# Tap spectra of a graph-network convolution with the cosine table stationary, and its scratch stored by frequency

## The chip, the core and the metric

The kernel runs on one core of one Trainium2 chip. The metric is device time in microseconds; the time before is the median of three runs. A profile is one further look at an execution by the hardware profiler: it records every instruction on every engine and every packet of a transfer. TensorE (PE), VectorE (DVE), ScalarE (ACT), GpSimd (POOL) and SyncE (SP) run side by side, each in the order of its own queue, and sixteen DMA engines move the data. Transfers are issued from SP's and ScalarE's queues.

## The reference, cut to what matters

```python
h = relu(layernorm(x))                     # x: 128 graphs x 128 nodes x 256 channels
xc = transpose(h, (0, 2, 1))
y = relu(bn1(conv1(xc)))                   # 1x1 convolution
y = bn2(conv2(y, pad=8))                   # 17 taps along the nodes, 256 -> 256 channels
x_conv = transpose(relu(y + xc), (0, 2, 1))
# message passing, a GRU cell on [x_conv, x_nmp] and h, residual
# a second layer: five small graph convolutions over subsets of 25 nodes, residual
```

The change concerns `conv2` alone, and of it the part that depends only on the weights: the spectrum of its 17 taps.

## The kernel before

`conv2` is done by spectra. Each graph's 128 nodes are cut into two windows of 80 (64 outputs and a margin of 8 on each side), so a spectrum has `LW = 80` real numbers: cosines and sines of 40 frequencies. The kernel computes the spectra of the inputs (X), the spectra of the taps (V, 80 x 256 x 256 numbers, 21 MB, written to the DRAM scratch `vd`), multiplies them frequency by frequency, and stores the products in `yd`, which a later stage turns back.

The work has these stages, for graphs in blocks of four (`BB`):

- Heads, for the first half of the graphs (`heads`, L266): for each block a load of x (`head_load`, L184), the statistics on VectorE (`head_stats`, L193 to L198), the normalisation (`head_norm`, L204), transposes on TensorE with ScalarE's eviction (`head_turn`, L214, L215, and a store of `htd` at L216), the 1x1 convolution (`head_conv1`, L228; VectorE L231, ScalarE L232) and the spectra of the block (`head_spectra`, L243, evicted at L249 and L251). Between these steps `some_spectra` (L376) adds one group of tap spectra at a time, two or three to a block.
- Tap spectra (`weight_spectra`, L160), only beside the heads of the first half. Taps come in tiles `w2` of 1 MB (`taps_load`, L152), eight of them, each for 128 input channels and 64 output channels, 17 taps on each of four groups of 32 partitions, the other 15 rows of a group being zeros in DRAM. A group of spectra is 16 matmuls (L167): 17 rows of taps are stationary, and the 80 columns of the cosine and sine table `gt` stream; four banks are filled, one per row group. ScalarE evicts three of them (L175), VectorE the fourth (L173; in the last group of a tile ScalarE takes all four). Four groups fill a tile `sp`, which ScalarE's queue stores into `vd` (L177).
- The products (`spectral`, L287), half by half: for every two frequencies a tile v is loaded by two transfers of 512 KB (L296), GpSimd adds its two parts (L311), TensorE multiplies (L304, L314, L319), and yd is stored from ScalarE's queue (L323).
- The rest (messages, gates, second layer), which the change doesn't touch. The only lines of it used below are the large stage's L649 (gates), L914 (500-column matmuls), L767 (a small transfer of 53 or 60 rows that lays a table of degrees out anew) and the loads of yr (L471).

What sets the order around the change: in the block from L362 to L409 the program order is kept on every engine as written (`tc.manual_schedule()`), so each engine runs the lines in the order of the calls. The taps of the first three tiles are loaded from SP's queue among the first loads of x; those of the further tiles are issued from ScalarE's queue (L383), each when the spectra of an earlier tile are done, just after the store of that tile and just before the copies of the next group. The tiles `w2` have three buffers and `sp` two. PSUM has eight banks, shared by all (`bank`, L93).

The lines that a sentence can't say:

```python
 167  nc.tensor.matmul(ps[r][:, j * LW:(j + 1) * LW], w2[32 * r:32 * r + KW, 4 * t + j, :],
 168                   gt[32 * r:32 * r + KW, :], start=True, stop=True)
 296  nc.sync.dma_start(v[:, c], vd[c, :, :, 2 * p:2 * p + 4, :].rearrange("q i d o -> i q d o"))
 380  if spectra and next(spectra[0], STOP) is STOP:
 381      spectra.pop(0)
 382      if len(todo) > 2:
 383          taps.append(taps_load(wp, *todo[2], nc.scalar))
```

Of the kernel before, what the change touches and what calls it, by code (L numbers as in the profile page):

```python
# [8 lines left out]
F32 = mybir.dt.float32  # L9
# [4 lines left out]
P = 128  # L14
EPS = 1e-5
KW = 17
# [3 lines left out]
OUTW = 64  # L20
LW = 80
NP_ = LW // 2
WCH = 64
NR = 2 * LW - P
PARTS = [40, 40, 40, 8]
NN = 25
# [49 lines left out]
def gnn_kernel(ctx: ExitStack, tc: tile.TileContext, io, out0: bass.AP, out1: bass.AP):  # L76
    nc = tc.nc
    x, adjT = io["x"], io["adjT"]
    B, N, D = x.shape
    C = D // P  # L80
# [9 lines left out]
    dram = ctx.enter_context(tc.tile_pool(name="dram", bufs=1, space=bass.MemoryType.DRAM))  # L90
    psum = ctx.enter_context(tc.tile_pool(name="psum", bufs=8, space=bass.MemoryType.PSUM))

    def bank():  # L93
        return psum.tile([P, 512], F32, tag="bank", name="bank")
# [6 lines left out]
    gt = hc.tile([P, LW], F32)  # L101
# [44 lines left out]


    htd = [dram.tile([P, C, T], F32, tag=f"ht{i}", name=f"htd{i}") for i in range(NBLK)]
    vd = dram.tile([C, D // WCH, P, LW, WCH], F32, tag="vd", name="vd")
    yd = [dram.tile([HG, 2, LW, D], F32, tag=f"yd{h}", name=f"yd{h}") for h in range(NH)]  # L150

    def taps_load(pool, c, q, queue, split=1, amid=None):  # L152
        w2 = pool.tile([P, WCH // 4, P], F32, tag="w2", name="w2", bufs=3)
        for t in range(0, WCH // 4, WCH // 4 // split):
            queue.dma_start(w2[:, t:t + WCH // 4 // split], io["w2t"][:, c, q, t:t + WCH // 4 // split])
            if amid:
                amid.pop()()
        return w2

    def weight_spectra(pool, c, q, w2):  # L160

        sp = pool.tile([P, LW, WCH], F32, tag="sp", name="sp", bufs=2)
        for t in range(WCH // 16):
            ps = [bank() for _ in range(4)]
            for j in range(4):
                for r in range(4):
                    nc.tensor.matmul(ps[r][:, j * LW:(j + 1) * LW], w2[32 * r:32 * r + KW, 4 * t + j, :],  # L167
                                     gt[32 * r:32 * r + KW, :], start=True, stop=True)
            for r in range(4):
                o0 = t * 16 + 4 * r  # L170
                dst, s = sp[:, :, o0:o0 + 4], ps[r][:, :4 * LW].rearrange("p (j d) -> p d j", j=4)
                if r == 3 and t < WCH // 16 - 1:
                    nc.vector.tensor_copy(dst, s)  # L173
                else:
                    nc.scalar.copy(dst, s)  # L175
            yield
        nc.scalar.dma_start(vd[c, q], sp)  # L177


    xs, stats, hcs, h1s = {}, {}, {}, {}  # L180
# [1 line left out]
    def head_load(pool, ahead, i, queue):  # L182
        xs[i] = pool.tile([P, BB, D], F32, tag="ln", name="ln", bufs=ahead)
        queue.dma_start(xs[i], x[i * BB:(i + 1) * BB].rearrange("b n d -> n b d"))  # L184
# [102 lines left out]
    def spectral(bp, X, h, amid):  # L287

        for p0 in range(0, NP_, 4):
            amid.get(p0, lambda: None)()  # L290
            ys = bp.tile([P, 4, 2, D], F32, tag="ys", name="ys", bufs=2)
            for p in range(p0, p0 + 4):
                if p % 2 == 0:
                    v = bp.tile([P, C, D // WCH, 4, WCH], F32, tag="v", name="v", bufs=3)
                    for c in range(C):
                        nc.sync.dma_start(v[:, c], vd[c, :, :, 2 * p:2 * p + 4, :].rearrange("q i d o -> i q d o"))  # L296
                vr, vi = v[:, :, :, 2 * (p % 2), :], v[:, :, :, 2 * (p % 2) + 1, :]
                a, d = X[:, :, p, 0, :], X[:, :, p, 1, :]
                y = ys[:, p - p0]
                ps = bank()  # L300
                if p == 0:
                    for k, (u, w) in enumerate(((a, vr), (d, vi))):
                        for c in range(C):
                            nc.tensor.matmul(ps[:, k * D:(k + 1) * D], u[:, c], w[:, c], start=c == 0, stop=c == C - 1)  # L304
                    nc.scalar.copy(y.rearrange("p k o -> p (k o)"), ps)
                    continue

                s = bp.tile([P, C, P], F32, tag="s", name="s", bufs=2)
                nc.vector.scalar_tensor_tensor(s, a, -2.0, d, op0=ALU.mult, op1=ALU.subtract)  # L309
                vs = bp.tile([P, C, D // WCH, WCH], F32, tag="vs", name="vs", bufs=3)  # L310
                nc.gpsimd.tensor_tensor(vs, vr, vi, op=ALU.add)  # L311
                p1 = bank()
                for c in range(C):
                    nc.tensor.matmul(p1[:, :D], a[:, c], vs[:, c], start=c == 0, stop=c == C - 1)  # L314
                k1 = bp.tile([P, D], F32, tag="k1", name="k1", bufs=2)
                nc.scalar.copy(k1, p1[:, :D])  # L316
                for k, (u, w) in enumerate(((s, vi), (d, vr))):
                    for c in range(C):
                        nc.tensor.matmul(ps[:, k * D:(k + 1) * D], u[:, c], w[:, c], start=c == 0, stop=c == C - 1)  # L319
                nc.vector.tensor_tensor(y, ps.rearrange("p (k o) -> p k o", k=2),  # L320
                                        k1[:, None, :].to_broadcast([P, 2, D]), op=ALU.add)
            for w in range(2):
                nc.scalar.dma_start(yd[h][:, w, 2 * p0:2 * p0 + 8, :].rearrange("g d o -> g (d o)"),  # L323
                                    ys[w * HG:(w + 1) * HG].rearrange("p a k o -> p (a k o)"))
# [29 lines left out]
    with front as es:  # L354
# [7 lines left out]
        with ExitStack() as ws:  # L362

            ws.enter_context(tc.manual_schedule())

            xk = ws.enter_context(tc.tile_pool(name="xk", bufs=1, side="right"))
            wp = ws.enter_context(tc.tile_pool(name="wp", bufs=1))
            ahead = 5
            todo = [(c, q) for c in range(C) for q in range(D // WCH)]
            nc.scalar.dma_start(gt, io["gt"])  # L370
            nc.scalar.dma_start(vec, io["vec"])

            taps = [taps_load(wp, *todo[0], nc.sync, split=4, amid=[lambda: head_load(xk, ahead, 0, nc.sync)])]
            spectra = []

            def some_spectra(k=1):  # L376
                for _ in range(k):
                    if not spectra and todo:
                        spectra.append(weight_spectra(wp, *todo.pop(0), taps.pop(0)))
                    if spectra and next(spectra[0], STOP) is STOP:  # L380
                        spectra.pop(0)
                        if len(todo) > 2:
                            taps.append(taps_load(wp, *todo[2], nc.scalar))  # L383
                        some_spectra()

            constant_loads()
            head_load(xk, ahead, 1, nc.sync)
            taps.append(taps_load(wp, *todo[1], nc.sync))
            for k in range(2, ahead):
                head_load(xk, ahead, k, nc.sync)  # L390
            nc.sync.dma_start(fw, row("fw", 5))
            taps.append(taps_load(wp, *todo[2], nc.sync))
            head_stats(hk, 0)
            some_spectra()
            head_norm(0)
            consts = constants()
            next(consts)
            some_spectra()
            some_spectra()
            head_turn(hk, 0)  # L400
            head_stats(hk, 1)
            some_spectra()
            next(consts)
            head_norm(1)
            head_stats(hk, 2)
            some_spectra()
            heads(hk, xk, ahead, X, 0, some_spectra)
            while spectra or todo:
                some_spectra()  # L409
        gw = ctx.enter_context(tc.tile_pool(name="gw", bufs=1, side="right", reuse_waits="tile"))  # L410
        xk = es.enter_context(tc.tile_pool(name="xk1", bufs=1, reuse_waits="tile"))
        bp = es.enter_context(tc.tile_pool(name="bp", bufs=1, reuse_waits="tile"))
# [15 lines left out]
        amid = {p: lambda: next(begin, None) for p in range(16, NP_, 4) if p != 20}  # L428
# [696 lines left out]
def _lay_out(a):  # L1125
# [3 lines left out]
    cc = np.ascontiguousarray  # L1129
# [4 lines left out]
    w = {k[7:]: v for k, v in a.items() if k.startswith("L0_gnn_")}  # L1134
    l = {k[7:]: v for k, v in a.items() if k.startswith("L1_gnn_")}
    d = {"x": cc(a["x"]), "xT": cc(a["x"].reshape(-1, BB * P, 2, P).transpose(0, 3, 2, 1)), "adjT": cc(a["adj"].transpose(0, 2, 1))}
# [2 lines left out]
        + [cols(w["b_ih"]), cols(w["b_hh"]), cols(l["b1"]), cols(l["b2"])], axis=1))  # L1139
    d["wc1"] = cc(w["conv1_w"][:, :, 0].T)  # L1140

    w2 = w["conv2_w"].reshape(-1, WCH // 16, 4, 4, 2, P, KW).transpose(2, 6, 4, 0, 1, 3, 5)
    d["w2t"] = np.zeros((4, 32) + w2.shape[2:], np.float32)
    d["w2t"][:, :KW] = w2
    d["w2t"] = d["w2t"].reshape(P, 2, -1, WCH // 4, P)
    d.update(_spectral_constants())
    pad = np.zeros((2 * MW - w["w_msg"].shape[0] - 3, w["w_msg"].shape[1]), np.float32)
    d["wms"] = cc(np.concatenate([w["w_msg"], w["w_se"], pad]).T)
# [16 lines left out]
    for g, (idx, ad) in enumerate(sub):  # L1165
        s = len(idx)
# [14 lines left out]
    for j, (k, (g, b0, nb)) in enumerate(PACKS):  # L1181
        s = len(sub[g][0])
# [27 lines left out]
```

## Time and profile before

| | |
|---|---|
| Runs, us | 1909.22, 1912.52, 1914.13 (median 1912.52) |
| Profiled execution, first to last instruction | 1904.7 us, TensorE clock 0.996 of full speed |
| Median of the runs less that span | 7.8 us |
| Busy, share of the span | PE 99%, PEld 86%, DVE 71%, ACT 38%, POOL 35% |
| Tap spectra L167, all 1024 records | 43.2 us of PE |
| Head pass of the first half | from 0 to about 161 us; last group of tap spectra at 124 us |
| HBM read, written | 178.66 MB, 85.14 MB |

The profiled execution's time outside its span isn't recorded on its own; 7.8 us is what the median of the runs stands above the span. How to read the profile: the rows of slices give each engine's busy share in tenths, DMA the mean over sixteen engines, so one busy engine alone is hardly seen in it. An fp32 matmul leaves two records, each with its own load of the stationary operand (PEld). The chain of waits follows the work back from the last instruction: each piece is what released the next. A window gives the busy time of every engine in a stretch; "(x241)" behind a time is a count of instructions.

### The profile page before, as it was taken

The page shows a single profiled execution, that of the slowest core. Times are in us where ns is not written, and L with a number is a line of the kernel's source. Part 1 is how long each engine was busy: PE and PEld are TensorE (multiplying, and loading weights), DVE is VectorE, ACT ScalarE, POOL GpSimd, SP SyncE. Part 2 cuts the span into 40 slices and gives each one's busy share as a digit, 9 for nine tenths or more (in the row PEclk, how much of TensorE's full clock was granted, in tenths as well). Part 3 has the DMA queues.
Part 4 walks back from the last instruction along what each step waited for, and adds up shares of the span by engine and source line. Part 5 has one row for each costly group of instructions (what it writes and reads, how often), then busy time and mean ns, then how long its engine had stood idle before and what let it go on. Part 6 is the DMA issues. An engine that isn't in the chain of part 4 may idle for free.

```text
span 1904.7 us, 31441 instructions
## 1 busy us (share of the span) xinstructions
PE 1881.7 (99%) x10994; PEld 1646.3 (86%) x10994; DVE 1345.3 (71%) x3246; ACT 723.9 (38%) x1588; POOL 667.7 (35%) x747
## 2 busy tenths in 40 slices
PE   9999999999999999999999999999999999999998
PEld 7889889988888888888888888888888888888887
DVE  6775558754778788887666777888666688787643
ACT  5552124411333433343343343343343434334334
POOL 1113431265335445444312244544322244444200
PEclk9999999999999999999999999999999999999999
DMA  9976995289732332233233433233234423222135
GB/s 349 328 295 221 306 321 206 100 286 315 235 89 73 97 87 73 73 98 97 73 106 96 131 89 85 73 88 108 81 89 101 137 74 108 65 78 72 36 92 152
DMA packets 248877, 265.87 MB, mean 140 GB/s; under 512 B 106866, under 2 KB 223943, under 8 KB 244239
## 3 DMA queue, kind: packets, MB, share of 16 engines
q1 hardware_dynamic: 238751, 199.82, 36.6%
q10 hardware_dynamic: 9968, 64.04, 8.6%
q8 instruction: 88, 1.44, 0.3%
q14 instruction: 70, 0.57, 0.1%
HBM read 178.66 MB, written 85.14 MB: 139 GB/s over the span
## 4 chain that ended last, share of the span: by engine, by line
PE 92%; DVE 3%; DMA 3%; POOL 1%; issue 1%; ACT 0%; SPq 0%; POOLq 0%; DVEq 0%; ACTq 0%
PE bank L649 45%; PE bank L319 6%; PE bank L974 5%; PE bank L535 5%; PE bank L914 5%; PE bank L228 4%; PE bank L314 3%; PE bank L600 3%; PE bank L243 3%; PE bank L512 3%; PE bank L167 2%; DMA v<-vd 1%; PE bank L515 1%; PE bank L893 1%; PE bank L214 1%; PE bank L825 1%
## 5 line engine op out<-in xcount | busy, mean ns | idle before, releaser
L649 PE MATMUL bank<-t,sw 128*128 128x256 f32 x1152 | 291.1, 380 | 0.0
L662 POOL TENSOR_TENSOR u<-u,m 128x256 f32<-128x256 f32 x128 | 94.8, 741 | 486.5 <-ACT m L660 442.4
L649 PEld LDWEIGHTS bank<-t,sw 128*128 128x128 f32 x1152 | 215.6, 190 | 29.6 <-issue 2.3
L649 PE MATMUL bank<-t,wih 128*128 128x256 f32 x768 | 197.2, 379 | 0.0
L649 PEld LDWEIGHTS bank<-t,wih 128*128 128x128 f32 x768 | 143.4, 190 | 19.3 <-issue 0.5
L311 POOL TENSOR_TENSOR vs<-v 128x512 f32<-128x512 f32 x78 | 101.4, 1320 | 113.5 <-DMA v<-vd 61.1
L228 PE MATMUL bank<-wc,ht 128*128 128x256 f32 x512 | 119.9, 387 | 1.4 <-ACT ht L215 1.4
L649 PE MATMUL bank<-t,whh 128*128 128x256 f32 x384 | 115.3, 382 | 2.8 <-DVE u L667 2.8
L649 PE MATMUL bank<-xc,wih 128*128 128x256 f32 x384 | 117.0, 386 | 0.7 <-DVE nh L664 0.2
L558 ACT ACTIVATE msg<-msg 128x512 f32<-128x512 f32 x64 | 36.8, 622 | 209.6 <-DVE msg L554 209.6
L974 PE MATMUL bank<-w,hh 128*125 128x256 f32 (+9 forms) x480 | 113.5, 380 | 1.5 <-DVE hh L919 1.5
L649 PE MATMUL bank<-xn,wih 128*128 128x256 f32 x384 | 114.2, 379 | 0.0
L228 PEld LDWEIGHTS bank<-wc,ht 128*128 128x128 f32 x512 | 97.0, 194 | 15.8 <-ACT ht L215 2.9
L649 PE MATMUL bank<-ht,whh 128*128 128x256 f32 x384 | 110.0, 380 | 0.0
L914 PE MATMUL bank<-ax,w 128*128 128x500 f32 (+8 forms) x416 | 106.9, 396 | 0.0
L198 POOL TENSOR_TENSOR rs<-ve,mhalf 128x4 f32<-128x4 f32 x32 | 32.8, 1026 | 205.5 <-DVE ve L196 205.5
L309 DVE SCALAR_TENSOR_TENSOR s<-X 128x256 f32<-128x256 f32 x78 | 49.9, 642 | 75.8 <-PE bank L319 75.2
L974 PEld LDWEIGHTS bank<-w,hh 128*125 128x125 f32 (+9 forms) x480 | 84.3, 177 | 19.8 <-DVE hh L919 1.9
L694 ACT ACTIVATE nn<-nn,vec 128x512 f32<-128x512 f32 x64 | 46.2, 722 | 135.0 <-DVE nn L693 135.0
L316 ACT COPY k<-bank 128x256 f32<-128x256 f32 x78 | 28.9, 373 | 171.8 <-DVE ys L320 79.7
L667 DVE TENSOR_TENSOR u<-bank,u 128x256 f32<-128x256 f32 x128 | 53.4, 417 | 57.7 <-PE bank L649 57.5
L649 PEld LDWEIGHTS bank<-xc,wih 128*128 128x128 f32 x384 | 70.5, 190 | 19.3 <-DVE nh L664 10.8
(207 smaller groups left out, 4537.6 us busy)
## 6 DMA issues: line engine op xcount, KB each, us to landing
v<-vd SPq DMA_DIRECT2D x80, 512.0 KB
vd<-sp ACTq DMA_DIRECT2D x8, 2560.0 KB
yd<-ys ACTq DMA_DIRECT2D x40, 512.0 KB
w<-in_w_dram SPq DMA_DIRECT2D x40, 512.0 KB
ln<-in_x_dram SPq DMA_DIRECT2D x32, 512.0 KB
htd<-ht ACTq DMA_DIRECT2D x32, 512.0 KB
ht<-htd SPq DMA_DIRECT2D x32, 512.0 KB
ym<-yd SPq DMA_DIRECT2D x32, 512.0 KB
```

The costliest lines, as they stand in the source:

```text
L228: nc.tensor.matmul(pv[:, bb, :], ht[:, c, b * N:(b + 1) * N], wc1[:, c, :], start=c == 0, stop=c == C - 1)
L243: nc.tensor.matmul(ps[:, bb * 2 * LW:(bb + 1) * 2 * LW], h1[:, 2 * h + bb, c * P:(c + 1) * P], fd, start=True, stop=True)
L311: nc.gpsimd.tensor_tensor(vs, vr, vi, op=ALU.add)
L314: nc.tensor.matmul(p1[:, :D], a[:, c], vs[:, c], start=c == 0, stop=c == C - 1)
L319: nc.tensor.matmul(ps[:, k * D:(k + 1) * D], u[:, c], w[:, c], start=c == 0, stop=c == C - 1)
L512: nc.tensor.matmul(ps[:, b * N:(b + 1) * N], ym[:, b, o * P:(o + 1) * P], idm, start=b == 0, stop=False)
L535: nc.tensor.matmul(ps[:, b, :], d[:, b * N:(b + 1) * N], w, start=True, stop=True)
L600: nc.tensor.matmul(ps[:, b * N:(b + 1) * N], msg[:, b, c * P:(c + 1) * P], e[:, b, :], start=True, stop=True)
L649: nc.tensor.matmul(ps, w, d, start=n == 0, stop=n == len(pairs) - 1)
L662: nc.gpsimd.tensor_tensor(got["u4"], got["u2"], got["m5"], op=ALU.add)
L914: nc.tensor.matmul(pv[:, q - q0, :], w1s[k5 + g][:, c, q * P:(q + 1) * P], xv[:, c], start=c == 0, stop=c == C - 1)
L974: nc.tensor.matmul(ps[:n1, :D], hh[:, q, at:at + n1], w2s[k5 + g][:, q, :], start=q == 0, stop=q == HID // P - 1)
```

## The change

The two operands of the tap spectra change places. The table `gt` (17 x 80 per row group) is stationary, and the taps stream, 512 columns (two input channels with 256 output channels each) on each of the four row groups. A group is four matmuls, which fill four banks of 80 x 512. Three are evicted by ScalarE and one by VectorE in each group. A tile of spectra now holds 16 input channels at all 80 frequencies, so there are 16 tiles of two groups each, and sp has three buffers. The scratch `vd` is stored by frequency, (80, 2, 128, 256), written from 80 partitions with 16 KB from each, and read by runs of 1 KB as before, now side by side. The taps lie in DRAM without the padded rows, by row group, tap, and pair of input channels; a tile `w2` (now [128, 2, 512]) is loaded by four transfers, one per row group, each 17 rows of 4 KB. So 8 stores of `vd` become 16, and the loads of taps, 11 transfers before (one tile in four pieces, seven whole), become 64, of which 12 are issued from SP's queue and 52 from ScalarE's. The rest of the kernel is the same.

```diff
-    vd = dram.tile([C, D // WCH, P, LW, WCH], F32, tag="vd", name="vd")
+    vd = dram.tile([LW, C, P, D], F32, tag="vd", name="vd")
...
-    def taps_load(pool, c, q, queue, split=1, amid=None):
-        w2 = pool.tile([P, WCH // 4, P], F32, tag="w2", name="w2", bufs=3)
-        for t in range(0, WCH // 4, WCH // 4 // split):
-            queue.dma_start(w2[:, t:t + WCH // 4 // split], io["w2t"][:, c, q, t:t + WCH // 4 // split])
-            if amid:
-                amid.pop()()
+    def taps_load(pool, u, queue):
+        w2 = pool.tile([P, 2, 512], F32, tag="w2", name="w2", bufs=3)
+        for r in range(4):
+            queue.dma_start(w2[32 * r:32 * r + KW], io["w2t"][r, :, 2 * u:2 * u + 2])
         return w2
 
-    def weight_spectra(pool, c, q, w2):
-
-        sp = pool.tile([P, LW, WCH], F32, tag="sp", name="sp", bufs=2)
-        for t in range(WCH // 16):
+    def weight_spectra(pool, u, w2):
+
+        c, i0 = divmod(2 * u * TI, P)
+        sp = pool.tile([P, 2 * TI, D], F32, tag="sp", name="sp", bufs=3)
+        for t in range(2):
             ps = [bank() for _ in range(4)]
-            for j in range(4):
-                for r in range(4):
-                    nc.tensor.matmul(ps[r][:, j * LW:(j + 1) * LW], w2[32 * r:32 * r + KW, 4 * t + j, :],
-                                     gt[32 * r:32 * r + KW, :], start=True, stop=True)
             for r in range(4):
-                o0 = t * 16 + 4 * r
-                dst, s = sp[:, :, o0:o0 + 4], ps[r][:, :4 * LW].rearrange("p (j d) -> p d j", j=4)
-                if r == 3 and t < WCH // 16 - 1:
-                    nc.vector.tensor_copy(dst, s)
+                g = slice(32 * r, 32 * r + KW)
+                nc.tensor.matmul(ps[r][:LW], gt[g, :], w2[g, t, :], start=True, stop=True)
+            for r in range(4):
+                dst = sp[:LW, t * TI + 2 * r:t * TI + 2 * r + 2, :].rearrange("d i o -> d (i o)")
+                if r == 3:
+                    nc.vector.tensor_copy(dst, ps[r][:LW])
                 else:
-                    nc.scalar.copy(dst, s)
-            yield
-        nc.scalar.dma_start(vd[c, q], sp)
+                    nc.scalar.copy(dst, ps[r][:LW])
+            yield
+        nc.scalar.dma_start(vd[:, c, i0:i0 + 2 * TI], sp[:LW])
...
-                    v = bp.tile([P, C, D // WCH, 4, WCH], F32, tag="v", name="v", bufs=3)
+                    v = bp.tile([P, C, 4, D], F32, tag="v", name="v", bufs=3)
                     for c in range(C):
-                        nc.sync.dma_start(v[:, c], vd[c, :, :, 2 * p:2 * p + 4, :].rearrange("q i d o -> i q d o"))
+                        nc.sync.dma_start(v[:, c], vd[2 * p:2 * p + 4, c].rearrange("d i o -> i d o"))
...
-            taps = [taps_load(wp, *todo[0], nc.sync, split=4, amid=[lambda: head_load(xk, ahead, 0, nc.sync)])]
+            taps = [taps_load(wp, todo[0], nc.sync)]
+            head_load(xk, ahead, 0, nc.sync)
...
                         if len(todo) > 2:
-                            taps.append(taps_load(wp, *todo[2], nc.scalar))
+                            taps.append(taps_load(wp, todo[2], nc.scalar))
...
-    d["w2t"] = np.zeros((4, 32) + w2.shape[2:], np.float32)
-    d["w2t"][:, :KW] = w2
+    d["w2t"] = cc(w["conv2_w"].transpose(2, 1, 0).reshape(KW, -1, 4, 2 * w["conv2_w"].shape[0]).transpose(2, 0, 1, 3))
```

More of the change, by code (lines that the diff above doesn't have):

```diff
@@ L22 @@
 NP_ = LW // 2
-WCH = 64
+TI = 8
 NR = 2 * LW - P
@@ L293, in spectral @@
                 if p % 2 == 0:
-                    v = bp.tile([P, C, D // WCH, 4, WCH], F32, tag="v", name="v", bufs=3)
+                    v = bp.tile([P, C, 4, D], F32, tag="v", name="v", bufs=3)
                     for c in range(C):
-                        nc.sync.dma_start(v[:, c], vd[c, :, :, 2 * p:2 * p + 4, :].rearrange("q i d o -> i q d o"))
-                vr, vi = v[:, :, :, 2 * (p % 2), :], v[:, :, :, 2 * (p % 2) + 1, :]
+                        nc.sync.dma_start(v[:, c], vd[2 * p:2 * p + 4, c].rearrange("d i o -> i d o"))
+                vr, vi = v[:, :, 2 * (p % 2), :], v[:, :, 2 * (p % 2) + 1, :]
                 a, d = X[:, :, p, 0, :], X[:, :, p, 1, :]
@@ L309, in spectral @@
                 nc.vector.scalar_tensor_tensor(s, a, -2.0, d, op0=ALU.mult, op1=ALU.subtract)
-                vs = bp.tile([P, C, D // WCH, WCH], F32, tag="vs", name="vs", bufs=3)
+                vs = bp.tile([P, C, D], F32, tag="vs", name="vs", bufs=3)
                 nc.gpsimd.tensor_tensor(vs, vr, vi, op=ALU.add)
@@ L368, in gnn_kernel @@
             ahead = 5
-            todo = [(c, q) for c in range(C) for q in range(D // WCH)]
+            todo = list(range(C * P // (2 * TI)))
             nc.scalar.dma_start(gt, io["gt"])
             nc.scalar.dma_start(vec, io["vec"])
-            taps = [taps_load(wp, *todo[0], nc.sync, split=4, amid=[lambda: head_load(xk, ahead, 0, nc.sync)])]
+            taps = [taps_load(wp, todo[0], nc.sync)]
+            head_load(xk, ahead, 0, nc.sync)
             spectra = []
@@ L378, in some_spectra @@
                     if not spectra and todo:
-                        spectra.append(weight_spectra(wp, *todo.pop(0), taps.pop(0)))
+                        spectra.append(weight_spectra(wp, todo.pop(0), taps.pop(0)))
                     if spectra and next(spectra[0], STOP) is STOP:
@@ L387, in gnn_kernel @@
             head_load(xk, ahead, 1, nc.sync)
-            taps.append(taps_load(wp, *todo[1], nc.sync))
+            taps.append(taps_load(wp, todo[1], nc.sync))
             for k in range(2, ahead):
@@ L391, in gnn_kernel @@
             nc.sync.dma_start(fw, row("fw", 5))
-            taps.append(taps_load(wp, *todo[2], nc.sync))
+            taps.append(taps_load(wp, todo[2], nc.sync))
             head_stats(hk, 0)
@@ L1140, in _lay_out @@
     d["wc1"] = cc(w["conv1_w"][:, :, 0].T)
-    w2 = w["conv2_w"].reshape(-1, WCH // 16, 4, 4, 2, P, KW).transpose(2, 6, 4, 0, 1, 3, 5)
-    d["w2t"] = np.zeros((4, 32) + w2.shape[2:], np.float32)
-    d["w2t"][:, :KW] = w2
-    d["w2t"] = d["w2t"].reshape(P, 2, -1, WCH // 4, P)
+    d["w2t"] = cc(w["conv2_w"].transpose(2, 1, 0).reshape(KW, -1, 4, 2 * w["conv2_w"].shape[0]).transpose(2, 0, 1, 3))
     d.update(_spectral_constants())
```

## The prediction

> **What bounds the kernel now.** I read the page first, then the chain of waits over the first 420 us, because every line of the change belongs to the first head pass, and then the engines by windows. Two rows of the page, 40 slices of 47.6 us each:
>
> ```profile
> PE   9999999999999999999999999999999999999998
> DMA  9976995289732332233233433233234423222135
> ```
>
> TensorE is busy throughout; the transfers are heavy only in the first ten slices. The page's chain is 92% TensorE. The chain in order of time (start, length, what), cut to the steps used below:
>
> ```profile
> 51.81 1.06 PE bank L167 x32
> ...
> 118.25 3.65 PE bank L228 x16
> 121.90 1.06 PE bank L167 x32
> ...
> 156.94 4.35 PE bank L243 x32
> 162.15 1.36 PE bank L304 x6
> ...
> 192.07 10.94 DMA v<-vd
> ```
>
> One group of tap spectra (16 matmuls, 32 records) takes 1.06 us of the chain. There are 32 groups; the one at 121.90 us is the 31st, the first that needs the last sixteenth of the taps in the new scheme. The heads end near 161 us. Until then nothing but TensorE's own order and short VectorE steps is on the chain; the waits for v come later. So the head pass is TensorE's, and its taps are there long before they are used (VectorE and ScalarE wait for L167's products, L167 for its taps only 0.4 us in all).
>
> Busy times by window (window, length, busy of PE, PEld, DVE, ACT, POOL with counts, clock, share of 16 DMA engines, GB/s):
>
> ```profile
> 24.00:131.00 107.00, 105.96 (x1294) 92.72 (x1293) 73.42 (x230) 62.95 (x172) 10.53 (x11) 1.00 0.86 319
> 525.10:525.48 0.38, 0.38 (x4) 0.33 (x3) 0.07 (x1) 0.14 (x1) 0.11 (x1) 1.00 0.07 20
> 525.52:525.80 0.28, 0.28 (x3) 0.25 (x2) 0.00 (x0) 0.00 (x0) 0.28 (x1) 1.00 0.41 110
> 154.00:156.00 2.00, 2.00 (x11) 1.77 (x10) 0.77 (x2) 0.13 (x1) 0.00 (x0) 1.00 0.46 186
> 168.00:170.00 2.00, 2.00 (x11) 1.77 (x10) 0.92 (x2) 0.37 (x1) 0.00 (x0) 1.00 1.04 366
> 132.00:138.00 6.00, 6.00 (x38) 5.54 (x37) 5.03 (x19) 2.33 (x8) 0.95 (x1) 1.00 1.01 430
> ```
>
> The second and third rows decide my forecast. At 525.1 us the transfer that runs is dvf<-dvt (L767), 53 rows of 512 bytes; the share is 0.07 of 16 engines, that is one engine, at 20 GB/s. A moment later a 60-row transfer of the same line runs, and the share is 0.41. A transfer of 53 rows, a prime, went through a single DMA engine. The last three rows give the speed of one engine: 4 KB rows (htd) 186/(0.46 x 16) = 25.3 GB/s, 1 KB rows 366/(1.04 x 16) = 22.0, 20 KB rows (vd) 430/(1.01 x 16) = 26.6.
>
> [...] 16 matmuls on four row groups take 1.06 us, where 8 matmuls of L228 with all rows take 3.65. [...] nothing in this trace has four groups with 512 columns.
>
> **The change part by part.**
>
> TensorE's groups. A group goes from 16 matmuls of 80 columns to 4 of 512, two records each. A 500-column record (L914) lasts 582 ns, a 256-column one (L228) 387, so a column costs (582-387)/244 = 0.80 ns and 512 columns 0.41 us. With four groups side by side it is two such passes one after the other, 0.82 us, and some 0.2 us to enter and leave: 1.0 us. Side by side not at all it would be 8 x 0.41 = 3.3 us. [...] I take 1.05, no change; the ends are -2 us and +72 us over 32 groups.
>
> Evictions. ScalarE did 104 copies of 320 columns, 37.3/104 = 0.359 us each in the group list; it gets 96 of 512. The nearest row is L215, 512 columns out of a bank, 36.3/64 = 0.567 us. That is 54.4 - 37.3 = +17 us on ScalarE. VectorE goes from 24 copies of 0.49 us to 32 of some 0.68 (L231): +10 us, on an engine with 73.42 of 107 us busy. The last copy of a block is now VectorE's, so ScalarE's store of the spectra may wait for it.
>
> Issues. ScalarE's queue issued 8 stores of vd and 5 tap loads; now 16 stores and 13 x 4 loads, 55 more. Small loads issued back to back stand 0.46 us apart (the yr loads at 477.9 and 478.4 us): +25 us of its queue. In the built program a set of four loads stands just before the copies of a new group; behind it wait these copies, behind them TensorE for its banks. The second to fourth load each also waits for an earlier transfer's semaphore. SP's queue issues 12 tap loads where it had 6, ahead of the x loads and fw; its 6 more issues cost 2.7 us, all before the taps themselves land.
>
> The tap loads. Padding goes: 8.39 MB become 64 x 69,632 bytes = 4.46 MB. Spread evenly, the 3.9 MB less would be worth 9 us of 16 engines at 26.6 GB/s each, and worth nothing here, since TensorE doesn't wait for taps. But each load is now 17 rows of 4 KB, and 17 is prime like 53: one engine[...]. At 25.3 GB/s it lasts 2.75 us; 64 last 176 us. In the kernel before, 1 MB of taps put 64 KB on each engine. This engine also carries its sixteenth of everything else, up to the last tap load: 13 stores of vd [...] at 81,920 bytes/26.6 = 3.08 us, 40 us; 15 x loads at 32,768/22.0 = 1.49, 22 us; 10 stores of htd at 32,768/25.3 = 1.30, 13 us; constants about 1.4. The sum is 252.4 us, from 1.7 us on. The last taps land at 254 and are used 0.6 us later (as with gt), at 254.7, where the group stood at 121.90: +132.8 us. Per sixteenth of the taps it is 11.0 + 3.1 + 1.0 + 1.2 = 16.3 us, where TensorE needs some 7.8 for the work beside it, so the engine doesn't run dry: three sets of taps are in flight or queued, and at most a few us of ScalarE's work stands between the end of one and the issue of another. All of the above (longer copies, issues, even groups of 3.3 us, 4.5 us more a set) lies beside these 16.3 us and costs nothing; if that cover is gone, it costs what the first rival says. What comes after the last taps (39.4 us to the end of the heads at 161.3) stays. TensorE will have idled and come back at half clock; after the 10.9 us wait at 192 the window from 200 to 220 us shows a clock of 0.91, that is 1.8 us lost, and I add 2.
>
> The new layout of vd. v is still read in runs of 1 KB, 512 to a transfer. The x loads already have runs that lie side by side, as v will; their windows move no faster than v's. I take 0 for the 26.8 us of waits for v between 192 and 284 us. The ends are -4 and +4 us, about a sixth either way. The products with v read 256 columns in one run instead of four: L314 (one run) and L319 (four) both last about 386 ns, 0.
>
> Sum: +133 + 2 = +135 us. The profiled span is 1904.7 us, which gives 2039.7; the median of the runs is 7.8 us above that span, so 2047.5, say 2047.
>
> **The rivals.** First: the rows are spread over several engines, and ScalarE becomes the bound. Its busy 63 us of 107, some 12 us of issues now (25 or so at 0.46), +17 and +25 make 117 us for 107: +10, 1922 us. For it speaks that ScalarE's queue is strictly in order; against it the 53-row transfer. Second, on the other side: the rows are spread and ScalarE keeps up because its issues run beside its copies. Then the place is the start: from 10.4 to 24.6 us TensorE runs at half speed (L228's 16 records take 6.27 us at 18.31 and 3.65 later). [...] the 6.27 fall by 2.6, the four groups of 1.94 among them in part by 1, the groups save 2: 1907. It decides from the point where a tap load lasts under about 1 us, so on three engines or more. Third: the row groups don't run side by side. With the taps spread that is +72, 1984; with one engine it is hidden, as said. Fourth, within the likeliest: less of the engine's other traffic lies ahead of the last taps. With half of it the last set lands at 216 us, which gives 2009; with a pause of 4 us in each of 16 sets it is 64 us more, 2111.
>
> **How the numbers follow.** One engine for the taps: 0.85. ScalarE's bound with spread taps 0.07, row groups in turn with spread taps 0.02, no difference of note 0.03, faster 0.03. A measurement of this kernel tells about 0.3% from no change. Slower is 0.85 + 0.07 + 0.02 = 0.94. The likeliest case's bounds, 2009 and 2111, leave out a little of it for packets that run faster or slower when one engine works alone; from 1985 to 2120 I give it 0.94 of its 0.85, which is the 0.8 wanted.
>
> **What would show it.** Right: in the first 270 us the DMA share falls to about a quarter while TensorE waits for w<-in_w2t; the loads are 17 rows, and L166's groups come in pairs 16 us apart; the first group starts near 13 us, not 4; a group still takes about 1.05 us once its taps are there; the spectral stage starts near 297 us, not 162. Wrong: a DMA share of 0.9 in the first 125 us with TensorE busy, which makes it a matter of ScalarE (its copies late, TensorE waiting for banks), or groups of 3 us.

## The result, and the profile after

| | before | after |
|---|---|---|
| Median of the runs, us | 1911.19 (1909.22 to 1914.13, 4 runs) | 2041.09 (2037.93 to 2048.82, 4 runs) |
| Ratio | | 1.0684, interval 1.0658 to 1.071 |
| Profiled span, us | 1904.7 | 2047.0 |
| TensorE clock | 0.996 | 0.972 |

The changed kernel takes 130 us longer, 6.8%. Forecast were 2047, with a range from 1985 to 2120.

Three rows of the page of the changed kernel, 40 slices of 51.2 us each. The heads of the first half fill nearly six of them, where they filled three and a half of 47.6:

```profile
PE   5786899999999999999999999999999999999998
PEclk9877799999999999999999999999999999999999
DMA  4454548873698333232342353323324443321225
```

Where TensorE was busy throughout, it is now idle for 66 of the first 256 us (about a quarter), its clock there is 0.83 in the mean, and the transfers are at 0.4 to 0.6 where the window from 24 to 131 us of the kernel before had 0.86. Less is moved, and it takes longer. After the fifth slice the rows are like those of before.

The chain of waits in order of time (start, length, what), over the first 420 us:

```profile
43.02 20.99 DMA w<-in_w2t_dram
...
147.77 19.33 DMA w<-in_w2t_dram
...
199.05 15.74 DMA w<-in_w2t_dram
214.81 21.49 DMA w<-in_w2t_dram
236.32 19.32 DMA w<-in_w2t_dram
...
255.77 1.96 PE bank L166 x2
...
259.63 1.94 PE bank L166 x8
...
295.50 4.35 PE bank L240 x32
...
331.23 11.66 DMA v<-vd
```

L166 is the new line of the tap matmuls, L240 that of the head spectra (L243 before). Up to 255.77 us the chain is mostly loads of taps, one behind the other. The matmul for the last of the taps, the fourth of the 31st group of tap spectra, starts at 255.77 us, where the whole group started at 121.90. (Each of the group's four matmuls waits for the load of its own row group alone: the first three were issued from 251.97 us on.) The first wait for v after the heads is about as long as before (11.66 beside 10.94 us).

Three windows (window, length, busy of PE, PEld, DVE, ACT, POOL, clock, DMA share, GB/s):

```profile
154.00:162.00 8.00, 4.16 (x14) 2.25 (x18) 1.98 (x5) 4.79 (x13) 0.00 (x0) 0.50 0.07 27
174.00:180.00 6.00, 5.62 (x11) 3.32 (x12) 2.85 (x10) 3.50 (x10) 0.43 (x1) 0.50 0.06 27
260.00:300.00 40.00, 40.00 (x234) 36.20 (x227) 25.68 (x77) 18.33 (x50) 6.76 (x6) 0.93 0.54 180
```

For 8 and for 6 us on end the share is 0.07 and 0.06 of sixteen engines: one engine, at 27 GB/s, while TensorE's granted clock is 0.50 and TensorE is, in the first of the two, idle for about half the time. This is the picture of the 53-row transfer of the kernel before (0.07, 20 GB/s), now with the taps. A mean share over sixteen engines shows such a bottleneck as idle transfers.

Where the difference comes in, by the end of each stage on TensorE, us:

| End of | before | after | difference |
|---|---|---|---|
| heads, first half | 161.3 | 299.9 | 138.6 |
| products, first half | 270.8 | 412.5 | 141.7 |
| heads, second half | 376.5 | 518.3 | 141.8 |
| products, second half | 479.4 | 621.4 | 142.0 |
| the kernel | 1904.7 | 2047.0 | 142.3 |

Of 142.3 us in the profiled executions, 138.6 arise in the stage that the change belongs to. These two executions lie further apart than the medians (129.9 us), because the profiled one of the changed kernel is the slowest of its four.

### The profile page after: what moved, and what is told of

The parts are those of the page before. It is cut to its first block, busy times and chain, and to the rows that moved or that the text cites. A ratio compares the mean times of both kernels' runs of the same rounds, so it can differ in the third digit from the quotient of the medians.

```text
span 2047.0 us, 30007 instructions
## 1 busy us (share of the span) xinstructions
PE 1959.4 (96%) x10226; PEld 1651.1 (81%) x10226; DVE 1356.4 (66%) x3254; ACT 734.4 (36%) x1580; POOL 666.7 (33%) x747
## 2 busy tenths in 40 slices
DMA packets 248824, 261.85 MB, mean 128 GB/s; under 512 B 106882, under 2 KB 223959, under 8 KB 244831
## 4 chain that ended last, share of the span: by engine, by line
PE 83%; DMA 11%; DVE 3%; issue 1%; POOL 1%; ACT 1%; ACTq 1%; SPq 0%; POOLq 0%; DVEq 0%
PE bank L647 43%; DMA w<-in_w2t_dram 8%; PE bank L316 6%; PE bank L972 5%; PE bank L533 5%; PE bank L912 5%; PE bank L311 3%; PE bank L598 3%; PE bank L225 3%; PE bank L510 3%; PE bank L240 2%; PE bank L513 1%; PE bank L891 1%; PE bank L823 1%; DMA ln<-in_x_dram 1%; DMA vd<-sp 1%
## 5 line engine op out<-in xcount | busy, mean ns | idle before, releaser
L166 PE MATMUL bank<-w,gt 17*80 17x512 f32 x256 | 93.0, 799 | 65.3 <-ACT sp L172 35.1
L308 POOL TENSOR_TENSOR vs<-v 128x512 f32<-128x512 f32 x78 | 101.3, 1317 | 117.5 <-DMA v<-vd 60.7
L225 PE MATMUL bank<-wc,ht 128*128 128x256 f32 x512 | 127.4, 405 | 1.4 <-ACT ht L212 1.4
L225 PEld LDWEIGHTS bank<-wc,ht 128*128 128x128 f32 x512 | 102.5, 205 | 25.9 <-ACT X L248 5.4
L166 PEld LDWEIGHTS bank<-w,gt 17*80 17x80 f32 x256 | 19.1, 173 | 107.4 <-ACT sp L172 51.3
L172 ACT COPY sp<-bank 80x512 f32<-80x512 f32 x96 | 49.9, 590 | 142.0 <-DMA w<-in_w2t_dram 63.2
L240 PEld LDWEIGHTS bank<-fd,h 128*128 128x128 f32 x512 | 86.9, 226 | 14.7 <-ACT ht L212 11.1
```

Of the source, the lines that this page charges most:

```text
L166: nc.tensor.matmul(ps[r][:LW], gt[g, :], w2[g, t, :], start=True, stop=True)
L225: nc.tensor.matmul(pv[:, bb, :], ht[:, c, b * N:(b + 1) * N], wc1[:, c, :], start=c == 0, stop=c == C - 1)
L240: nc.tensor.matmul(ps[:, bb * 2 * LW:(bb + 1) * 2 * LW], h1[:, 2 * h + bb, c * P:(c + 1) * P], fd, start=True, stop=True)
```

## The experiments

The theory was: a load of 17 rows goes through one DMA engine, and this engine's sum of packets sets when the last taps land. The first rival: the rows are spread, and ScalarE's queue is the bound (longer copies, 52 loads to issue). The rows of a load tell them apart without a change in the instructions, since rows beyond 17 are zeros that no matmul reads.

### Rows in a load: 32, 23, 25, and one load of 128

The versions with four loads a tile differ from the changed kernel in the rows of a load and the zeros in DRAM, here with 32:

```diff
-            queue.dma_start(w2[32 * r:32 * r + KW], io["w2t"][r, :, 2 * u:2 * u + 2])
+            queue.dma_start(w2[32 * r:32 * r + 32], io["w2t"][r, :, 2 * u:2 * u + 2])
...
+    d["w2t"] = np.zeros((4, 32) + w2.shape[2:], np.float32)
+    d["w2t"][:, :KW] = w2
```

Four loads of 32 rows:

> The changed kernel with one edit: each of the four tap loads of a tile takes 32 rows (17 and 15 rows of zeros) in place of 17, so twice the bytes, the same 64 loads from the same queues. If the loss is one DMA engine carrying all taps, 32 rows go over 16 engines, a load costs 8 KB on each and the taps stop being late: 1915 to 1930 us, with no wait for w over 2 us after the first. If the loss is ScalarE's queue (64 small loads to issue and longer copies), nothing changes: 2035 to 2050 us.

Measured: 1989.3 us, ratio 1.0422 (1.0405 to 1.044). Both expectations missed. With 88% more bytes a load the kernel is 52 us faster than with 17 rows, but 80 us slower than before. So something second lies under the first. The chain of e1_rows32 around one block shows it:

```profile
98.31 0.32 ACTq L174
98.63 0.04 ACT X L248
98.67 5.29 DMA w<-in_w2t_dram
103.95 0.04 issue
104.00 1.55 ACT sp L172 x3
```

ScalarE issues the store of the spectra (L174, 1.31 MB), then stands 5.3 us in four loads of taps, and only then makes the three copies that TensorE's banks wait for. The four issue records at this place last 0.44, 2.03, 2.17 and 0.53 us; each waits for the landing of an earlier transfer before it, but for the second and third these had landed by 97.7 us, so that their 2 us are not this wait. All 52 have this minimum, median and maximum in ns:

```profile
L155 ACTq DMA_DIRECT2D w<-in_w2t_dram x52: 317/1222/2572, 16.9 to 183.9; - x52
```

Thirteen such blocks at 5.3 us would be 69 of the 80 us, an estimate; the section after this one puts it to the test.

One load of 128 rows a tile, all zeros included:

```diff
-        for r in range(4):
-            queue.dma_start(w2[32 * r:32 * r + 32], io["w2t"][r, :, 2 * u:2 * u + 2])
+        queue.dma_start(w2, io["w2t"][:, 2 * u:2 * u + 2])
```

> The changed kernel with padded taps and one load of 128 rows for a tile in place of four, so 16 loads for 64, on 16 engines. One-engine theory: as with 32 rows, less the issue time of 39 loads on ScalarE's queue; 1908 to 1925 us. ScalarE theory: here too the time falls, to 1915 us or so, but with 32 rows it would not have. The difference to the kernel with four loads of 32 rows is the price of the issues; I expect 5 to 10 us.

Measured: 1920.9 us, ratio 1.0064 (1.0045 to 1.0083). The time was as expected; that it lies 68 us under e1_rows32 was not. The same bytes in a quarter of the issues: what e1_rows32 loses goes with the number of loads. In this kernel ScalarE's issues of taps have a median of 0.47 us:

```profile
L154 ACTq DMA_DIRECT2D w<-in_w2t_dram x13: 346/472/2469, 15.7 to 118.4; - x13
```

Four loads of 23 rows, prime like 17, and of 25 rows, which five divides (that the divisors of the rows set the number of engines was the author's assumption; the kernel before had shown 53 rows at a share of 0.07 and 60 rows at 0.41):

> The changed kernel with 23 rows in each tap load (6 rows of zeros): 23 is prime, so again one engine, with 6/17 more for it to carry. One-engine theory: 64 x 6 x 4096 bytes at 25.3 GB/s is 62 us more than the changed kernel, 2095 to 2110 us. If bytes or issues in all decide, 1.6 MB more over 16 engines is 4 us: 2041 to 2050.

> The changed kernel with 25 rows in each tap load: more bytes than with 23, but 25 divides by 5, so five engines take 5 rows each. One-engine theory: 64 x 5 x 4096 bytes at 25.3 GB/s is 52 us on each of the five engines beside some 75 us of other traffic, about 127 us, where TensorE needs 122 for the same stretch: near the kernel with 32 rows, 1915 to 1940 us. If padding bytes cost, it is slower than with 23 rows.

Measured: 23 rows 2102.12 us, ratio 1.1011 (1.0994 to 1.1027), as the one-engine sum had it (61 us over 17 rows, where 62 were worked out). 25 rows 1981.92 us, ratio 1.0387 (1.037 to 1.0404): not the 1915 to 1940 expected, but with two rows more than 23 it is 120 us faster. The last head spectra of the first half start here in 23 rows,

```profile
346.01 4.35 PE bank L240 x32
```

and here in 25 rows:

```profile
234.46 4.35 PE bank L240 x32
```

No instruction of an engine differs between the two but the rows of the loads.

The pages also let the engines be counted. These are the lines on packets for 17, 23, 25 and 32 rows:

```profile
DMA packets 248824, 261.85 MB, mean 128 GB/s; under 512 B 106882, under 2 KB 223959, under 8 KB 244831
DMA packets 249208, 263.42 MB, mean 125 GB/s; under 512 B 106882, under 2 KB 223959, under 8 KB 245215
DMA packets 249593, 263.95 MB, mean 133 GB/s; under 512 B 107139, under 2 KB 224216, under 8 KB 245600
DMA packets 250744, 265.79 MB, mean 134 GB/s; under 512 B 107842, under 2 KB 224919, under 8 KB 246751
```

The rows of the taps are 4 KB each, so none of them is among the packets under 512 bytes. Yet 64 loads of 25 rows have 257 of these small packets more than 64 loads of 17 (4 a load, and one besides), 64 loads of 32 rows have 960 more (15 a load), and 64 loads of 23 rows none. The added ones are packets of four bytes, which stand in the trace where a load ends. If every engine that takes part in a load leaves one of them, and 17 rows use one engine, then 23 rows use one, 25 rows five and 32 rows sixteen. This settles the first limit. And 25 and 32 rows come out within 8 us of each other; that the second limit holds both is likely, but it is tested below with 32 rows alone.

### Who issues the loads

If ScalarE's standing is the second limit, issuing from SP's queue removes it. In the 32-row version:

```diff
-                            taps.append(taps_load(wp, todo[2], nc.scalar))
+                            taps.append(taps_load(wp, todo[2], nc.sync))
```

> The padded version with four loads of 32 rows a tile, 1.042 of the kernel before, with one edit: its 13 tap loads of the loop (four transfers each) are issued by SyncE's queue in place of ScalarE's. If what is left above the kernel before is ScalarE standing some 5.5 us a tile in the issue of four loads behind its own 1.28 MB store of spectra, with its copies and TensorE's banks behind it, the time falls by 55 to 70 us, to 1915 to 1935 us. If it is the transfers (how long four loads of 32 rows take to land) or the longer copies, the time stays within 10 us of 1989.

Measured: 1930.37 us, ratio 1.0121 (1.0102 to 1.014), 59 us less than e1_rows32. The issues themselves are still long at times (minimum, median, maximum in ns):

```profile
L155 SPq DMA_DIRECT2D w<-in_w2t_dram x64: 310/566/2959, 0.7 to 128.7; - x64
```

An issue of up to 2.96 us now holds SP, where no copy waits behind it. In SP's queue there is no store of spectra, so the standing isn't tied to sharing a queue with that store.

The same edit in the changed kernel, with its 17 rows:

> The changed kernel with one edit: the tap loads of the loop are issued by SyncE's queue in place of ScalarE's. If one DMA engine that carries every row of the taps sets the pace (252 us of packets before the last taps land), who issues them is of no account: 2025 to 2045 us, the last group of taps at 240 to 258 us. If the standing ScalarE queue is what the change costs, the time falls to under 1990.

Measured: 2040.38 us, ratio 1.0706 (1.0683 to 1.0729): within the interval of the changed kernel, as the theory of one engine had it. Its chain ends the heads like this:

```profile
232.23 23.25 DMA w<-in_w2t_dram
...
255.62 1.05 PE bank L166 x2
...
290.56 4.35 PE bank L240 x32
```

The last taps are used at 255.6 us, as at 255.8 in the changed kernel. With 17 rows ScalarE's standing was hidden beside the one engine; it costs nothing measurable there, and some 59 us where the rows are spread.

### The old kernel with unpadded taps

Only the storing and loading of the taps is changed in the kernel before:

```diff
-            queue.dma_start(w2[:, t:t + WCH // 4 // split], io["w2t"][:, c, q, t:t + WCH // 4 // split])
+            for r in range(4):
+                queue.dma_start(w2[32 * r:32 * r + KW, t:t + WCH // 4 // split], io["w2t"][r, :, c, q, t:t + WCH // 4 // split])
```

(The first tile is loaded in one piece of four loads, not in four.)

> The kernel before with only its taps stored without padding and loaded as four transfers of 17 rows of 8 KB a tile: its own spectra matmuls, copies and layout of the spectra. If the unpadded rows alone make the change's cost, this is about as slow as the change: worked out by the same sum the last tile's taps land near 237 us where they are used at 113, so +124, 2020 to 2050 us. If the cost lies in the new order of the spectra (stationary cosines, 512-column copies, stores by frequency), it stays within 20 us of 1910.

Measured: 2057.11 us, ratio 1.0784 (1.0758 to 1.081), 7 us above the expected range and slower than the whole change. Its chain:

```profile
153.20 31.00 DMA w<-in_w2t_dram
184.23 32.98 DMA w<-in_w2t_dram
...
303.88 4.35 PE bank L244 x32
```

So the unpadded rows alone bring all of the loss to the old order of spectra too; new matmuls, copies and layout are not needed for it. That it comes out higher than the sum (some 20 us later at the end of the heads) stays open.

### Unpadded taps on sixteen engines

The taps stay unpadded in DRAM; SP's queue issues the loads, 16 rows at a time and the four seventeenth rows together:

```diff
         for r in range(4):
-            queue.dma_start(w2[32 * r:32 * r + KW], io["w2t"][r, :, 2 * u:2 * u + 2])
+            queue.dma_start(w2[32 * r:32 * r + 16], io["w2t"][r, :16, 2 * u:2 * u + 2])
+        queue.dma_start(w2[16:P:32], io["w2t"][:, 16, 2 * u:2 * u + 2])
```

> The changed kernel with its taps still unpadded in DRAM, loaded from SyncE's queue (2040 us with four loads of 17 rows) as four loads of 16 rows and one load of the four seventeenth rows. The bytes are the same. If the one DMA engine that takes all rows of a 17-row load is the cost, rows in sixteens take all 16 engines and the time is near that of 32 rows from the same queue, 1915 to 1935 us. If it is the small transfers or the missing padding as such, it stays above 1990.

Measured: 1928.45 us, ratio 1.0096 (1.008 to 1.0112): 112 us less than e6_rows17_sp with the same bytes and one transfer more a tile. Missing padding as such costs nothing, and gains nothing measurable over the padded e5_rows32_sp (1.0121). The small packets of its page fit as well: 107,907 under 512 bytes are 1025 more than with 17 rows, 15 for each of the 64 loads of 16 rows, 4 for each of the 16 loads of four rows, and one besides. The same window of the changed kernel and of e10_rows16_1_sp:

```profile
24.00:131.00 107.00, 77.45 (x254) 42.06 (x254) 36.26 (x106) 29.17 (x62) 5.03 (x5) 0.88 0.45 141
24.00:131.00 107.00, 104.66 (x569) 68.39 (x562) 74.77 (x213) 66.49 (x148) 10.07 (x10) 0.97 0.91 275
```

TensorE is busy 104.66 of 107 us instead of 77.45, and the transfers stand at 0.91 instead of 0.45.

### The last 0.6%

One load of 128 rows a tile, from SP's queue (the same edit as in e5_rows32_sp):

> The padded version with one load of 128 rows a tile, 1.0064 of the kernel before, with its loop's tap loads issued by SyncE's queue in place of ScalarE's. There one load stood 2.4 us in ScalarE's queue at some tiles, and TensorE waited for banks behind it. If that wait is the rest of the difference, this is 1906 to 1914 us, no slower than the kernel before; if the longer copies of ScalarE (68 us busy of 107 beside 63) or the stores' 512-byte-longer runs and the half-clocked start make it, it stays at 1916 to 1925.

Measured: 1920.07 us, ratio 1.0068 (1.0042 to 1.0094). The wait behind a single issue was not the rest. Its chain at the start and at the end of the heads:

```profile
14.05 4.20 PE bank L165 x8
...
162.74 4.35 PE bank L239 x32
```

The heads end 5.8 us later than before, and another 3.5 us come up to the end of the products of the second half (488.7 us where it was 479.4), which no run here explains. In the heads two places were seen: ScalarE makes no copy between 10.1 and 15.6 us, since its first store stands in its queue until VectorE has made the tile's last copy, and TensorE's group at 14.05 us takes 4.20 us (the next one, at 20.25, takes 1.94) because it waits for banks; and 7 of the 32 groups (the first expectation below says 8) take 1.83 to 1.87 us instead of 1.03, since their last two banks wait for ScalarE's third copy. Each was tried:

```diff
-                if r == 3:
+                if r >= 2:
```

> The padded version with one load of 128 rows a tile from SyncE's queue, 1.0068 of the kernel before, with two of each group's four bank copies on VectorE and two on ScalarE, where it was one and three. In its trace 8 of the 32 groups of tap spectra take 1.83 to 1.87 us instead of 1.03, each right after a round of head spectra: the third and fourth of their banks wait for ScalarE's third copy of the group before. If that wait is what is left of the difference, these groups fall to 1.0 to 1.3 us and the time falls by 4 to 7 us, to 1906 to 1911. If VectorE (80 us busy of 107, and some 18 more now) becomes late instead, the time stays or rises, up to 1930.

Measured: 1925.4 us, ratio 1.0083 (1.0067 to 1.01). No gain. Of the waits of the first 180 us (who waits, for what, us in total, times, longest), e8_whole128_sp has this line for the load of the head spectra's stationary operand:

```profile
PEld bank L239 <- ACT sp L171: 6.4, 8, 0.8
```

and e9_whole128_sp_22 has this one:

```profile
PEld bank L239 <- DVE sp L169: 8.4, 5, 1.7
```

VectorE's copies stand in its queue behind the normalisation of a block (1.29 us in the chain), and TensorE waits for these. The wait changed engines.

```diff
-        nc.scalar.dma_start(vd[:, c, i0:i0 + 2 * TI], sp[:LW])
+        nc.sync.dma_start(vd[:, c, i0:i0 + 2 * TI], sp[:LW])
```

> The padded version with one load of 128 rows a tile from SyncE's queue, 1.0068 of the kernel before, with the 16 stores of the spectra issued by SyncE's queue as well. In its trace ScalarE stands 6.6 us at the first of these stores, from 8.59 to 15.24 us, until VectorE has made the last copy of the block; its copies of the next group wait behind it, and TensorE for banks. TensorE is 3.9 us late by 35 us, and only 2.0 us more from there to the last group. If that stand is the cause, the stage of the heads ends 3 to 4 us earlier, near 163 us instead of 167, and the time falls to 1913 to 1918. If SyncE now holds the loads behind it up by as much, or the start is late because the first group has twice the matmul length on half speed, the heads end near 167 as before and the time stays at 1918 to 1924.

Measured: 1920.15 us, ratio 1.0063 (1.0042 to 1.0084). No gain either. The start is 1 us earlier (the group that began at 35.55 us begins at 34.35), but the loads of taps, now behind stores and loads of x in one queue, come late twice in the chain of the profiled execution, which at 1928.16 us is the slowest of its six:

```profile
43.96 17.91 DMA w<-in_w2t_dram
...
97.66 16.46 DMA w<-in_w2t_dram
...
173.76 4.35 PE bank L239 x32
```

What makes the last 0.6% is therefore not settled beyond these places: several waits of a few us, of which one grew when another was taken away. Nor is the end of the heads in a single profile a sure guide to so small a difference: it is 173.8 us in e2_whole128, 167.1 in e8_whole128_sp and 178.1 in e11_whole128_allsp, whose medians lie within 1 us of each other. No version tried was faster than the kernel before.

## Why the prediction was right, point by point

- **One engine for the taps.** Right, and shown: by the windows at a share of 0.06 to 0.07, by 23 against 25 rows (2102.12 and 1981.92 us), and by 17 rows against 16 and 1 (2040.38 and 1928.45 us). That 17 rows would go as the 53 had gone was the author's estimate from that one transfer; the times and the small packets with 17, 23, 25 and 32 rows agree with it (one, one, five and sixteen engines). That the one engine is always the same was an estimate too, which the sum rests on; the traces don't record which engine took a packet. In one stretch of the changed kernel they agree with it: from 173.7 to 179.9 us the packets stand one behind the other, first the 4 KB packets of taps, 0.16 us each, then five of 16 KB of a store of vd, 0.61 us each, at a share of 0.06 in all.
- **The sum of that engine's packets.** 254.7 us was predicted for the use of the last taps and 255.77 measured: +133.9 us where +132.8 was worked out. In the two windows above a single engine ran at 27 GB/s, not 25.3. A packet of the stores of vd took 0.82 us in the median of all engines for 16 KB, where I had reckoned 0.62 (16 KB at 26.6 GB/s); in the stretches where one engine was at work alone it took 0.61. The two errors are of opposite sign, but what the stores took on the busy engine in all can't be told from the trace (that a store puts five of its 80 rows on it, as the sum has it, agrees with the small packets, 106,866 before and 106,882 after: 64 loads with one each, eight stores more and 11 loads of 128 rows less with sixteen each make the 16 between them); that the sum hit to 1 us is partly luck. From 2 to 255.7 us only one stretch of over 0.1 us, of 0.53 us, has no packet at all. This fits an engine that doesn't run dry, as the sum has it, without proving it.
- **After the last taps.** I added 2 us for half clock to an unchanged 39.4. It was 44.1 to the end of the heads, +4.7: the matmuls of both groups after the last taps still took 1.96 and 1.94 us, at a granted clock of 0.50 from 255.77 to 261.57 us, and the clock was 0.93 from 260 to 300 us. (In the kernel before it was 0.57 from 204 to 208 us, behind the wait of 10.94 us for v.)
- **Groups.** An undisturbed group took 1.03 us in e2_whole128 and e8_whole128_sp (1.05 taken, 1.06 before). Four row groups with 512 columns do run side by side: in turn they had been estimated at 3.3 us, and side by side at 1.0.
- **Copies.** ScalarE's 96 copies took 0.52 us each (49.9/96), not 0.567: +12.6 us in the sum, not +17. Hidden here, as forecast. The groups of the changed kernel (line, shapes, count, busy us, mean ns, idle time before and what ended it):

```profile
L166 PE MATMUL bank<-w,gt 17*80 17x512 f32 x256 | 93.0, 799 | 65.3 <-ACT sp L172 35.1 <-DMA w<-in_w2t_dram 30.1
L172 ACT COPY sp<-bank 80x512 f32<-80x512 f32 x96 | 49.9, 590 | 142.0 <-DMA w<-in_w2t_dram 63.2 <-issue 23.8 <-PE bank L166 22.5
```

  Read on their own, these lines name ScalarE as the first cause of TensorE's idle time, 35.1 us. But e6_rows17_sp, which takes the loads off ScalarE, is no faster: ScalarE waited for the taps itself.
- **Issues, and with them the first rival.** This is the term that was mis-sized. I took 0.46 us for each load, from small loads issued one after another, and let ScalarE's sum of busy times decide: 1922 if the rows were spread. With the rows spread it was 1982 and 1989. An issue took 1.05 and 1.22 us in the median and over 2 us at worst, and what counts isn't the sum of ScalarE's work but the 5.3 us on end in which no copy is made. In the changed kernel this was hidden, so the number didn't suffer; had the load had 25 rows, the forecast for that case would have been 60 us too low.
- **Layout of vd.** 0 was taken: the idle time of GpSimd before its sum of v, ended by loads of v, is 60.7 us after and 61.1 before, and the products of the second half take as long (103 us each). The products of the first half took 3.1 us longer, inside the -4 to +4 given; TensorE's work there is the same (105.8 us busy beside 106.4), and nearly all of the difference is one stop of 2.99 us at 373 us, for which the trace shows no cause.
- **From the span to the runs.** I added 7.8 us, the median over the profiled span. The runs of the changed kernel stand 1.8 us above their own spans, so most of the 7.8 was a difference between executions. In the profiled one the span was 2047.0, where 2039.7 was forecast: 1 us from the sum, 3 from the stretch after the last taps, 3 from the first products.
- **Signs.** The first spectral stage started at 299.9 us (near 297 forecast), and from pair to pair of groups it was 16.4 us in the mean (16 forecast), but unevenly, from 8 to 27. Three signs were off. The DMA share was about half in the long slices, and 0.07 only in the pauses, where a quarter was forecast. The first group started at 6.4 us and not near 13, because its first matmul needs one of the four loads; the last of the four started near 14.8. And a group whose taps were there took about 1.1 us in some cases (1.10 at 102.83 us, at a granted clock of 1.00) but 1.9 to 2.0 us in others (2.01 at 259.56 us, at 0.50). The sum rests on none of the three. The second and third rivals are out: the groups run side by side, and nothing at the start is faster (the eight records of L138 took 2.08 us in both kernels, and a matmul of the taps, two records, still took 1.96 us at 56.82 us, as at 6.44).

## What to carry to other kernels

Before the bytes of a load are cut, look at how many rows it has left: 17, 23 or 53 rows, primes all, went through one DMA engine here, where 25 rows went through five and 32 through sixteen by their small packets, and the same bytes moved as 16 rows and 1 made this kernel 112 us faster than as 17. Read a low mean share of the DMA engines beside a chain made of one transfer as a question, not as spare room: 0.06 of sixteen was one engine at work without a pause here, at 27 GB/s. And count what an engine stands still while it issues, in one piece, where its next work is what TensorE's banks wait for; a load that is moved to a queue without copies cost 59 us less.

## What the runs showed that I had not expected

- The issue of a load isn't of a fixed price. The same 32-row load took 0.31 us at least and 2.96 us at most to issue from SP's queue, and 0.32 to 2.57 us from ScalarE's. In e1_rows32 the second and third of four, right after a store of 1.31 MB, took 2.03 and 2.17 us. That it happens on SP as well, whose queue holds no such store, speaks against a cause in the queue itself; what inside the issue takes the time, these runs don't tell.
- The packets of a store have no fixed speed. In the changed kernel 16 KB of a store of vd took from 0.61 to 2.00 us, 0.82 in the median (20 GB/s on an engine), and in e8_whole128_sp 0.61 in the median; the 20 KB of the kernel before ran at 26.6 GB/s. What sets this isn't shown.
- In the changed kernel the granted clock was 0.50 in both windows with one engine at work, where TensorE waited up to 5.61 us at a time, and 0.50 from 255.77 to 261.57 us, where it no longer waited; over the whole kernel it fell from 0.996 to 0.972. What sets it isn't shown.
